# The per-query maxima of an fp32 attention block: from transposes on TensorE to 32x32 squares on VectorE, with one part of the conditioning moved inside the front

## The chip, the cores and the metric

The kernel runs on one core of one Trainium2 chip. The metric is the device time of one execution in microseconds (us), taken as the median of the runs. Everything is computed in fp32.

## The reference

One transformer block with adaptive layer norm, on x of shape (2, 2048, 576) with 16 heads of 36 channels and a hidden width of 2304:

```python
ada = silu(c) @ W_ada + b_ada                       # six parts of 576, one row per batch
shift_msa, scale_msa, gate_msa, shift_mlp, scale_mlp, gate_mlp = jnp.split(ada, 6, axis=-1)
h = modulate(layernorm(x), shift_msa, scale_msa)    # x * (1 + scale) + shift
qkv = h @ W_qkv + b_qkv
attn = softmax((q * 36**-0.5) @ k.T)                # per head, 2048 x 2048
x = x + gate_msa * ((attn @ v) @ W_proj + b_proj)
h = modulate(layernorm(x), shift_mlp, scale_mlp)
x = x + gate_mlp * (gelu(h @ W_fc1 + b_fc1) @ W_fc2 + b_fc2)
```

## The kernel before

**The front** (lines 174 to 592) computes queries, keys and values of batch 0 in four stages of 512 tokens (`queries_keys_values`). Each stage is a generator: its matmuls stand in half-steps between `yield`s (a query/key pair `pq` of two 128-column groups is two half-steps, a value tile `pv` is one). Between the half-steps one step of another generator, `later` (line 517), is taken. `later` works off what is not needed at once: parts 2, 5, 3 and 4 of the conditioning. Part 2 is `gate_msa`, the third of the six. For a part, `load_ada` brings 576 columns of `W_ada` to SBUF (tile `wa`, DMAs on SyncE's queue), `cleared` zeroes a PSUM tile `pa` with VectorE, `rows_of` (line 418) multiplies (line 425) and copies out, and `gates` spreads the row over 128 partitions by two more matmuls (line 475). After that `later` scales the projection and MLP weights by the gates (`gated`, DMAs on GpSimd's queue).

**The main part** is one loop over slots `G` (line 1332), in an order written out by hand: every instruction of compute is kept in program order on its engine. A round (class `Unit`, number u) is one head with 512 queries: 8 blocks of 512 queries x 16 heads = 128 rounds. A round has four groups of 512 keys (NG = 4), one group per slot, and g = G mod 4 is the slot's place in its round. A slot issues, in this order:

- `scores` of the round two rounds ahead (AHEAD = 8 slots): 8 matmuls into two PSUM tiles `s` (line 648; the pool `ps_s` has two), and `keep`, two ScalarE copies of them to SBUF tiles `e` (line 661).
- `fill`: other matmul work, one or two steps at a time, chosen by a running credit: projections of batch 1 (`pq_q`, `pv_q`), the output projection of a finished block (`po`), the MLP (`pf`, line 1172, and `py`, line 1220). Their last matmuls on 64 rows (line 104) are held back as `lasts`.
- `exps`: one ScalarE exponential over a group of the next slot (line 707).
- `weigh`: 8 matmuls of probabilities with values into the PSUM tile `av` (line 719). The pool `ps_v` holds one `av`, so the first `weigh` of a round (g = 0) waits until the previous round's `av` has been read.
- `maxima`: VectorE joins the group's scores into a running maximum `acc` (line 666), one or two `tensor_max` of 1,024 elements; in the last group a third of 512 elements (recorded under line 666 too) joins the two halves, and `acc[:, :512]` then holds, for each of 128 partitions, a maximum per query.
- `less`: VectorE subtracts the maximum `m` from a group (line 703, 2,048 elements), two slots ahead of its `weigh`; it is what `subtract(G + 2)` calls.
- `done`s: what takes the filled PSUM tiles out, on VectorE or ScalarE.
- at g = 3, `take` (lines 731 and 732): ScalarE copies the first half of `av` to `up`, VectorE adds the second half. This is what sets `av` free.

The 128 partition maxima of a query must still be joined. `turn` (line 678) does four TensorE transposes of 128x128 into a third `s` tile, called `mt`; `across` (line 691) reduces them with VectorE (`mx`, line 694), sends 2 KB to DRAM (`m_d`, line 695) and reads them back to all partitions (`m`, line 698), both on SyncE's queue. The two stand in the slot after the last group, g = 0, which the loop calls the chain slot: the order there is subtract, `turn`, `lasts`, `weigh`, `across`, maxima. At g = 2 the maxima stand ahead of the subtract, in the other slots after it.

Of the kernel before, what the change touches and what calls it, by code (L numbers as in the profile page):

```python
# [10 lines left out]
F32 = mybir.dt.float32  # L11
AF = mybir.ActivationFunctionType
ALU = mybir.AluOpType
AX = mybir.AxisListType
# [3 lines left out]
P = 128  # L18
# [4 lines left out]
def dit_block_kernel(  # L23
# [16 lines left out]
    nc = tc.nc  # L40
# [9 lines left out]
    QB = 512  # L50
    NQB = L // QB
    TB = QB // P
# [4 lines left out]
    NG = HALF // (2 * P)  # L57

    def seq(ins):

        return tc.keep_in_program_order(ins)
# [112 lines left out]
    with ExitStack() as front:  # L174
# [200 lines left out]
        def load_in(n):  # L375
# [141 lines left out]
        def later():  # L517

            was[2] = load_ada(2)
            was[5] = load_ada(5)  # L520
            lines = ap.tile([P, C], F32, name="lines")
            for b in range(B):
                for i, src in enumerate((b_fc2, b_proj)):
                    at = ds(64 * b + 32 * i, 1)
                    seq(nc.gpsimd.dma_start(out=lines[at, :], in_=src.unsqueeze(0)))
            yield
            yield
            yield
            pas[2] = cleared(2)
            yield  # L530
            g1 = []
            yield from gates(2, g1)
            was[3] = load_ada(3)
            pas[5] = cleared(5)
            yield
            g2 = []
            yield from gates(5, g2)
            was[4] = load_ada(4)
            half = [ap.tile([P, C], F32, name=f"half_{b}") for b in range(B)]
            for b in range(B):  # L540
# [26 lines left out]
            t = rows_of(4)  # L567
            yield
            modulation(4, t)()
# [27 lines left out]
    NU = NB * H  # L597

    with ExitStack() as main_part:
# [3 lines left out]
        ps_s = pool("ps_s", 2, space=PSUM)  # L603
# [3 lines left out]
        np_ = pool("n", 2)  # L607
# [4 lines left out]
        class Unit:  # L612
# [50 lines left out]
            def maxima(self, g):  # L663

                one, two = (self.es[g][:, j].rearrange("p i n -> p (i n)") for j in range(2))
                top = lambda out, x, y: seq(nc.vector.tensor_max(out, x, y))  # L666
                if g == 0:
                    self.acc = np_.tile([P, 2 * QB], F32, tag="acc", name=f"acc_{self.u}", bufs=1)
                    top(self.acc, one, two)
                    return  # L670
                a = self.acc
                top(a, a, one)
                top(a, a, two)
                if g == NG - 1:
                    self.am = a[:, :QB]
                    top(self.am, a[:, :QB], a[:, QB:])

            def turn(self):

                room = ps_s.tile([P, 2, 512], F32, tag="s", name=f"mt_{self.u}")  # L680
                self.pt = room[:, 0, :].rearrange("p (i n) -> p i n", i=TB)
                for i in range(TB):
                    seq(
                        nc.tensor.transpose(  # L684
                            self.pt[:, i, :],
                            self.am.rearrange("p (n i) -> p i n", i=TB)[:, i, :],
                            ident,
                        )
                    )

            def across(self):

                mx = np_.tile([P, TB], F32, tag="mx", name=f"mx_{self.u}")
                seq(nc.vector.tensor_reduce(out=mx, in_=self.pt, op=ALU.max, axis=AX.X))  # L694
                seq(nc.sync.dma_start(out=m_d[self.u], in_=mx))
                self.m = np_.tile([P, QB], F32, tag="m", name=f"m_{self.u}")
                flat = m_d[self.u].rearrange("p i -> (p i)")
                seq(nc.sync.dma_start(out=self.m, in_=flat.partition_broadcast(P)))

            def less(self, g):  # L700
# [590 lines left out]
        units = [Unit(u) for u in range(NU)]  # L1291
        AHEAD = 2 * NG
# [19 lines left out]
        def subtract(G):  # L1312
            if 0 <= G < NU * NG:
                units[G // NG].less(G % NG)
# [17 lines left out]
        for G in range(-AHEAD, NU * NG + 1):  # L1332
            u, g = divmod(G, NG)
            state["slot"] = G

            su, sg = divmod(G + AHEAD, NG)
            if sg == 0 and su + 1 < NU:
                units[su + 1].load_keys()
            if g == 1 and -1 <= u and u + 1 < NU:
                units[u + 1].load_values()  # L1340
            cu, cg = divmod(G - 1 + AHEAD, NG)
            chain = cg == NG - 1 and 0 <= cu < NU
            count(RATE)
            forced = g % 2 == 0 or G < 0 or credit > RATE
            tiles = units[su].scores(sg) if su < NU else None
# [8 lines left out]
            if 0 <= G + 1 < NU * NG:  # L1354
                lu, lg = divmod(G + 1, NG)
                units[lu].exps(lg)
            if chain:
                subtract(G + 2)
                units[cu].turn()
            for last in lasts:  # L1360
                last()
            lasts.clear()
            if 0 <= G < NU * NG:
                units[u].weigh(g)
            if chain:
                units[cu].across()
                if tiles:
                    units[su].maxima(sg)
            elif g == NG - 2:
                if tiles:  # L1370
                    units[su].maxima(sg)
                subtract(G + 2)
            else:
                subtract(G + 2)
                if tiles:
                    units[su].maxima(sg)
# [76 lines left out]
```

## Time and profile before

| | |
|---|---|
| median of 3 runs | 3703.63 us (3703.1 to 3707.89) |
| the profiled execution | 3707.24 us, span 3705.5 us |
| busy in the span | PE 3682.3, PEld 1722.0, DVE 2948.0, ACT 2327.3, POOL 706.2 us |
| granted TensorE clock | 0.999 of full speed |
| front, up to the first scores | 269.7 us |
| mean round, from one `mx` to the next | 24.73 us, of which VectorE is busy 21.49 us |
| tail after the last `mx` | 265 us |

PE is TensorE's matmuls, PEld its weight loads, DVE VectorE, ACT ScalarE, POOL GpSimd, SP SyncE. A row of a timeline is: start in us, length in us, engine, line, operation, written tile <- read tiles, shapes, and xN for N instructions merged into one row; in brackets the idle time of the engine ahead of it, and what ended it. An fp32 matmul appears as two instructions. The start of the next row tells what a row costs its engine, since rows overlap at their ends.

### The profile page before, as it was taken

To read this page: it belongs to the slowest core of one execution; us is meant where nothing else is said; L and a number is where in the kernel's file an instruction comes from. 1 tells how busy PE (TensorE), PEld (TensorE's weight loads), DVE (VectorE), ACT (ScalarE), POOL (GpSimd) and SP (SyncE) were. 2 spreads that over 40 slices of the span, in tenths; PEclk is the share of its full clock that TensorE was granted. 3 is DMA by queue.
4 is the path that set the end of the run, shared out by engine and by line. 5 is a ranking of instruction groups with operands and counts; after the bars stand their busy time and mean duration, and the time that the engine had idled before them with its cause. 6 is when DMAs were issued, how large, how long until landed. Compare 5 with 4: busy or idle time off the path is not lost.

```text
span 3705.5 us, 59239 instructions
## 1 busy us (share of the span) xinstructions
PE 3682.3 (99%) x23926; PEld 1722.0 (46%) x23926; DVE 2948.0 (80%) x3000; ACT 2327.3 (63%) x2166; POOL 706.2 (19%) x1044
## 2 busy tenths in 40 slices
PE   8999999999999999999999999999999999999999
PEld 4554344444444534454444444453444444444565
DVE  4627889889888888888889888988889888988422
ACT  0006767668776677667667777767667767676321
POOL 0101121222122111311131212211130213111411
PEclk9999999999999999999999999999999999999999
DMA  7733333544244343524353424424352435342522
GB/s 245 267 110 105 100 99 96 119 116 111 67 109 112 76 90 80 126 66 99 79 133 70 113 65 114 108 60 105 76 126 67 99 82 120 80 97 61 136 71 70
DMA packets 426946, 382.13 MB, mean 103 GB/s; under 512 B 315591, under 2 KB 316633, under 8 KB 426673
## 3 DMA queue, kind: packets, MB, share of 16 engines
q0 software_dynamic: 77248, 205.28, 20.5%
q1 hardware_dynamic: 82928, 129.54, 12.5%
q10 hardware_dynamic: 266496, 43.53, 7.2%
q8 instruction: 189, 3.10, 0.4%
q14 instruction: 85, 0.69, 0.1%
HBM read 306.98 MB, written 71.21 MB: 102 GB/s over the span
## 4 chain that ended last, share of the span: by engine, by line
PE 94%; DMA 3%; DVE 1%; ACT 1%; issue 1%; POOL 0%; SPq 0%; DVEq 0%; ACTq 0%; POOLq 0%
PE av L719 23%; PE s L648 22%; PE py L1220 15%; PE pf L1172 14%; PE po L799 4%; PE pq_q L975 3%; PE pq L278 3%; PE pf L104 2%; PE pv L328 2%; PE pv_q L799 2%; PE mt L684 2%; DMA x_b<-gp_d 1%; PE po L104 1%; DMA wa<-in_L_cond_W_ada_dram 1%; DVE acc L666 0%
## 5 line engine op out<-in xcount | busy, mean ns | idle before, releaser
L661 ACT COPY e<-s 128x1024 f32<-128x1024 f32 x1024 | 990.2, 1025 | 813.3 <-PE s L648 802.7
L703 DVE TENSOR_TENSOR e<-e,m 128x2048 f32<-128x2048 f32 x512 | 1162.8, 2276 | 9.8 <-DMA m<-m_d 9.8
L666 DVE TENSOR_TENSOR acc<-acc,e 128x1024 f32<-128x1024 f32 x768 | 939.5, 1223 | 171.9 <-ACT e L661 127.7
L707 ACT ACTIVATE e<-e 128x2048 f32<-128x2048 f32 x512 | 991.2, 1936 | 0.9 <-DVE e L703 0.8
L719 PE MATMUL av<-e,v 64*64 64x512 f32 x8192 | 981.3, 594 | 0.1
L648 PE MATMUL s<-qT,kT 36*64 36x512 f32 x8192 | 973.4, 589 | 2.1 <-DVE mx L694 1.1
L1220 PE MATMUL py<-w,gT 128*128 128x288 f32 x2304 | 580.2, 410 | 0.0
L648 PEld LDWEIGHTS s<-qT,kT 36*64 36x64 f32 x8192 | 313.1, 133 | 571.3 <-issue 522.8
L719 PEld LDWEIGHTS av<-e,v 64*64 64x64 f32 x8192 | 296.0, 133 | 510.0 <-issue 460.3
L1172 PE MATMUL pf<-h_b,w_b 128*128 128x512 f32 x1152 | 530.7, 605 | 0.0
L1220 PEld LDWEIGHTS py<-w,gT 128*128 128x128 f32 x2304 | 432.4, 190 | 175.4 <-issue 37.2
L740 POOL DMA_DIRECT2D o_d<-up x128 | 109.3, 854 | 1969.8 <-DMA o_d<-up 1439.2
L1172 PEld LDWEIGHTS pf<-h_b,w_b 128*128 128x128 f32 x1152 | 208.2, 190 | 318.0 <-issue 303.7
L694 DVE TENSOR_REDUCE mx<-mt 128x4 f32<-128x512 f32 x128 | 88.2, 689 | 169.9 <-PE mt L684 169.9
L1183 ACT ACTIVATE gT<-pf,bias 128x512 f32<-128x512 f32 x144 | 99.1, 688 | 193.0 <-PE pf L104 132.7
L1192 DVE SCALAR_TENSOR_TENSOR th<-th,gT 128x1024 f32<-128x1024 f32 x72 | 88.1, 1223 | 90.0 <-ACT th L1190 89.8
L666 DVE TENSOR_TENSOR acc<-e 128x1024 f32<-128x1024 f32 x128 | 155.6, 1216 | 4.4 <-ACT e L661 4.4
L1232 DVE TENSOR_TENSOR x_b<-py,x_b 128x288 f32<-128x288 f32 x192 | 81.5, 452 | 84.2 <-PE py L1220 84.2
L741 POOL DMA_DIRECT2D sum_d<-up x128 | 144.0, 1125 | 1.0 <-issue 1.0
L799 PE MATMUL po<-wpr_p,oT 128*128 128x288 f32 x512 | 132.6, 413 | 0.0
L278 PE MATMUL pq<-hT,w_in 128*128 128x512 f32 (+1 forms) x320 | 129.2, 555 | 0.0
L766 POOL DMA_DIRECT2D w_b<-in_L_cond_W_fc_dram x72 | 73.8, 1025 | 266.9 <-PE pf L1172 242.9
(156 smaller groups left out, 2453.2 us busy)
## 6 DMA issues: line engine op xcount, KB each, us to landing
w<-w_d POOLq DMA_DIRECT2D x72, 576.0 KB, 6.1
v<-v_d ACTq DMA_DIRECT2D x128, 296.0 KB
kT<-qk_d SPq DMA_DIRECT2D x256, 144.0 KB
w_b<-in_L_cond_W_fc_dram POOLq DMA_DIRECT2D x72, 512.0 KB, 4.6
m<-m_d SPq DMA_DIRECT2D x128, 256.0 KB
qT<-qk_d SPq DMA_DIRECT2D x256, 72.0 KB
w_d<-wg POOLq DMA_DIRECT2D x12, 864.0 KB, 8.4
qk_d<-ev SPq DMA_DIRECT2D x36, 256.0 KB
```

What stands on the lines that cost most here:

```text
L104: nc.tensor.matmul(outs[r][ts(c, 64), :], lhsT=lefts[r][:, ts(c, 64)], rhs=rights[r], start=starts[r], stop=not starts[r],)
L278: nc.tensor.matmul(pq[:, r, :n], lhsT=w_in[:, kc, cols], rhs=hT[:, kc, at], start=(kc == 0 and not (two and r)), stop=(kc == KC - 2 and tw ...
L648: nc.tensor.matmul(s[ts(c, 64), i, :], lhsT=self.kT[at, ds((2 * g + j) * P + 64 * c, 64)], rhs=self.qT[at, :], start=True, stop=True,)
L661: seq(nc.scalar.copy(self.es[g][:, j], s))
L666: top = lambda out, x, y: seq(nc.vector.tensor_max(out, x, y))
L703: seq(nc.vector.tensor_sub(e, e, m))
L707: seq(nc.scalar.activation(e, e, AF.Exp))
L719: nc.tensor.matmul(self.av[ts(i, 64), r, :], lhsT=self.v[ts(r, 64), ds((c + i * (HALF // P)) * HA, 64)], rhs=e[ts(r, 64), j, i, :], start= ...
L741: seq(nc.gpsimd.dma_start(out=sums, in_=hi[0:1, :], accum_op=ALU.add))
L799: nc.tensor.matmul(outs[n][:, :C2], lhsT=src[:, kc, ts(i, P)], rhs=w_[:, kc, ts(n, C2)], start=(kc == 0), stop=False,)
L1172: nc.tensor.matmul(pfs[j], lhsT=wc[:, kc, ts(j, P)], rhs=h2[:, kc, :], start=(kc == 0 and j == 0), stop=(kc == KC - 2 and j == 1),)
L1220: nc.tensor.matmul(py[n][:, :C2], lhsT=gTs[f - f % 2][:, f % 2, ts(i, P)], rhs=w2s[f - f % 2][:, f % 2, ts(n, C2)], start=(j == 0), stop=( ...
```

## The change

`turn` and the chain slot go. `maxima` calls `across` itself as soon as the last group is joined, at g = 3, ahead of `take`. `across` now does everything on VectorE, inside the tile `acc`:

```diff
                 if g == NG - 1:
-                    self.am = a[:, :QB]
-                    top(self.am, a[:, :QB], a[:, QB:])
+                    top(a[:, :QB], a[:, :QB], a[:, QB:])
+                    self.across(a)
...
-            def turn(self):
-                room = ps_s.tile([P, 2, 512], F32, tag="s", name=f"mt_{self.u}")
-                self.pt = room[:, 0, :].rearrange("p (i n) -> p i n", i=TB)
-                for i in range(TB):
-                    seq(nc.tensor.transpose(self.pt[:, i, :],
-                        self.am.rearrange("p (n i) -> p i n", i=TB)[:, i, :], ident))
-            def across(self):
-                mx = np_.tile([P, TB], F32, tag="mx", name=f"mx_{self.u}")
-                seq(nc.vector.tensor_reduce(out=mx, in_=self.pt, op=ALU.max, axis=AX.X))
-                seq(nc.sync.dma_start(out=m_d[self.u], in_=mx))
+            def across(self, a):
+                v = a[:, QB:].rearrange("p (i n) -> p i n", n=32)
+                seq(nc.vector.transpose(v, a[:, :QB].rearrange("p (n i) -> p i n", n=32)))
+                n16 = QB // 32
+                mq = a[:, :n16]
+                seq(nc.vector.tensor_reduce(out=mq, in_=v, op=ALU.max, axis=AX.X))
+                m4 = a[:32, n16 : 5 * n16].rearrange("p (r i) -> p r i", r=4)
+                for r in range(4):
+                    seq(nc.vector.tensor_copy(m4[:, r], mq[ts(r, 32), :]))
+                mx = np_.tile([32, n16], F32, tag="mx", name=f"mx_{self.u}")
+                by_query = m4.rearrange("p r i -> p i r")
+                seq(nc.vector.tensor_reduce(out=mx, in_=by_query, op=ALU.max, axis=AX.X))
+                flat = m_d[self.u].rearrange("p i -> (p i)")
+                seq(nc.sync.dma_start(out=flat.rearrange("(n i) -> n i", n=32), in_=mx))
                 self.m = np_.tile([P, QB], F32, tag="m", name=f"m_{self.u}")
-                flat = m_d[self.u].rearrange("p i -> (p i)")
                 seq(nc.sync.dma_start(out=self.m, in_=flat.partition_broadcast(P)))
```

The transpose turns each 32x32 square by itself, so that each quarter of 32 partitions comes to hold its own maximum of query 16p + i in partition p. Four copies bring the quarters side by side into the first 32 partitions, and a last reduction over four joins them. In the loop, `chain`, the early subtract of the chain slot and the two calls are taken out:

```diff
-            if chain:
-                subtract(G + 2)
-                units[cu].turn()
             for last in lasts:
                 last()
...
-            if chain:
-                units[cu].across()
-                if tiles:
-                    units[su].maxima(sg)
-            elif g == NG - 2:
+            if g == NG - 2:
```

In the front, `later` has two more `yield`s ahead of `pas[2] = cleared(2)`, so that part 2, and all that follows it in `later`, stands two half-steps later:

```diff
             yield
             yield
             yield
+            yield
+            yield
             pas[2] = cleared(2)
```

On the queues this moves, in each round, the store of the maxima and the read back: on SyncE they now stand ahead of the next `load_keys` (tiles `kT`, `qT`) instead of behind it. On VectorE, `take`'s add (line 732) now stands behind `across`. On TensorE only the transposes leave; in the front the ten matmuls of part 2 move behind two half-steps of `pq`, and those of parts 5, 3 and 4 move with them.

More of the change, by code (lines that the diff above doesn't have):

```diff
@@ L674, in maxima @@
                 if g == NG - 1:
-                    self.am = a[:, :QB]
-                    top(self.am, a[:, :QB], a[:, QB:])
-            def turn(self):
-                room = ps_s.tile([P, 2, 512], F32, tag="s", name=f"mt_{self.u}")
-                self.pt = room[:, 0, :].rearrange("p (i n) -> p i n", i=TB)
-                for i in range(TB):
[L683 to L689, printed above, removed]
-            def across(self):
-                mx = np_.tile([P, TB], F32, tag="mx", name=f"mx_{self.u}")
-                seq(nc.vector.tensor_reduce(out=mx, in_=self.pt, op=ALU.max, axis=AX.X))
-                seq(nc.sync.dma_start(out=m_d[self.u], in_=mx))
+                    top(a[:, :QB], a[:, :QB], a[:, QB:])
[14 more added lines that the diff above has]
+                seq(nc.sync.dma_start(out=flat.rearrange("(n i) -> n i", n=32), in_=mx))
                 self.m = np_.tile([P, QB], F32, tag="m", name=f"m_{self.u}")
-                flat = m_d[self.u].rearrange("p i -> (p i)")
                 seq(nc.sync.dma_start(out=self.m, in_=flat.partition_broadcast(P)))
@@ L1340, in dit_block_kernel @@
                 units[u + 1].load_values()
-            cu, cg = divmod(G - 1 + AHEAD, NG)
-            chain = cg == NG - 1 and 0 <= cu < NU
             count(RATE)
```

## The prediction

> **What bounds the kernel now.** I read the page's busy times and its chain of waits first, then the groups that the change touches, and then the timelines of TensorE and VectorE around the end of a round, since shares over the whole span cannot say what a stage is worth.
>
> ```profile
> PE 3682.3 (99%) x23926; PEld 1722.0 (46%) x23926; DVE 2948.0 (80%) x3000; ACT 2327.3 (63%) x2166; POOL 706.2 (19%) x1044
> PE av L719 23%; PE s L648 22%; PE py L1220 15%; PE pf L1172 14%; PE po L799 4%; PE pq_q L975 3%; PE pq L278 3%; PE pf L104 2%; PE pv L328 2%; PE pv_q L799 2%; PE mt L684 2%; DMA x_b<-gp_d 1%; PE po L104 1%; DMA wa<-in_L_cond_W_ada_dram 1%; DVE acc L666 0%
> L694 DVE TENSOR_REDUCE mx<-mt 128x4 f32<-128x512 f32 x128 | 88.2, 689 | 169.9 <-PE mt L684 169.9
> ```
>
> TensorE is the chain nearly everywhere, and the transposes `mt` are on it. VectorE's 80% looks like room, but between 300 and 3440 us it is busy 2728.7 of 3140 us, 87%, and the idle time in front of the removed reduction is no room that TensorE grants: it is VectorE waiting for the transposes.
>
> TensorE around the end of two rounds, first at 2004 to 2024 us, then at 1755 us:
>
> ```profile
> 2006.26 4.15 PE L799 MATMUL po<-wpr_p,oT 128*128 128x288 f32 x16
> 2010.25 0.63 PE L684 MATMUL mt<-ident,acc 128*128 128x128 f32 x4
> 2010.81 0.72 PE L104 MATMUL po<-wpr_p,oT 64*64 64x288 f32 x8
> 2011.34 1.90 PE L719 MATMUL av<-e,v 64*64 64x512 f32 x16
> ...
> 2018.33 4.15 PE L799 MATMUL po<-wpr_p,oT 128*128 128x288 f32 x16
> 2022.40 0.72 PE L104 MATMUL po<-wpr_p,oT 64*64 64x288 f32 x8
> ...
> 1759.09 0.63 PE L684 MATMUL mt<-ident,acc 128*128 128x128 f32 x4
> 1759.65 1.95 PE L719 MATMUL av<-e,v 64*64 64x512 f32 x16
> ```
>
> VectorE at the same two places:
>
> ```profile
> 2007.54 0.69 DVE L666 TENSOR_TENSOR acc<-acc 128x512 f32<-128x512 f32 x1
> 2008.15 0.68 DVE L732 TENSOR_TENSOR up<-up,av 128x512 f32<-128x512 f32 x1
> ...
> 1755.24 0.69 DVE L666 TENSOR_TENSOR acc<-acc 128x512 f32<-128x512 f32 x1
> 1755.85 0.68 DVE L732 TENSOR_TENSOR up<-up,av 128x512 f32<-128x512 f32 x1
> 1756.45 2.28 DVE L703 TENSOR_TENSOR e<-e,m 128x2048 f32<-128x2048 f32 x1
> 1759.76 0.69 DVE L694 TENSOR_REDUCE mx<-mt 128x4 f32<-128x512 f32 x1 [1.02 <-PE mt L684]
> ```
>
> The reader is to see two things. With transposes the way from `po` to its last matmuls takes 4.55 us (2006.26 to 2010.81), without them 4.07 us (2018.33 to 2022.40). And the add that sets `av` free, L732, ends at 2008.83, and TensorE needs `av` at 2011.34: 2.51 us of slack now. The change puts `across` into just this gap.
>
> **TensorE's transposes, removed.** 0.48 us per round (4.55 - 4.07) x 128 = 61.4 us; the chain's own share, 1.6% of 3705.5, says 59. With them go waits of TensorE at the third `s` tile: 3.0 us for `acc`, 1.9 us for ScalarE's copies, 1.1 us of `s` behind `mx`, together 6.0 us. Nothing takes their place on TensorE.
>
> **The front.** TensorE waits for part 2's weights:
>
> ```profile
> 34.00 3.70 PE L278 MATMUL pq<-hT,w_in 128*128 128x512 f32 x8
> 40.81 3.66 PE L425 MATMUL pa<-wa,cT 128*2 128x288 f32 x20 [3.11 <-DMA wa<-in_L_cond_W_ada_dram]
> ...
> 59.33 2.11 PE L425 MATMUL pa<-wa,cT 128*2 128x288 f32 x20
> ```
>
> 3.11 us ahead of them, and the matmuls stretch to 3.66 us where part 5's take 2.11: 4.7 us in all. In the new order two half-steps of `pq` come first, some 7 to 8 us of work (44.40 to 49.31, and a second half-step of 3.5), so from 37.7 TensorE reaches part 2 at about 45.5, when the weights, used up by 44.4 before, are there. Its cover is that `w_in`'s columns have landed: they were issued at 10 to 14 us, `wa`'s at 29. If not, the wait only moves, and the gain is nil. The later steps of `later` slide by two half-steps; what they prepare (scaled weights, the last two parts) is first read hundreds of us on, and the DMAs keep their order on each queue. I take 4.7 us, bounds 0 and 4.7.
>
> **VectorE's chain, added.** The links wait for each other, so their full lengths count. No row shows a transpose on VectorE. Of 512 elements, one source: the like-sized rows take 0.69 us (the half join, L694); two elements at a time, from the 128x128 copy of 222 ns, would make it 0.42; each element twice, 1.22 (the 1,024-element rows). I take 0.69, the row of the same size. The reduction of 512 to 16: 0.69, as L694. Four copies of 32x16: six small writes of `mod` (L458) stand in 0.79 us, 0.13 each, and a dependent small step in the `rstd` chain costs 0.20; so 0.5 to 1.0, taken 0.60. The last reduction: 0.16 for the smallest row (L397) and about 56 more elements, 0.22. Four hand-overs of 0.03, less the 0.08 by which a following independent row starts early: together 2.3 us from the end of the join to the start of the add, bounds 1.7 and 3.3.
>
> Against it stands the reduction removed, 0.60 us start to start, but that stood behind the add. So VectorE's work grows by 1.7 us a round: 21.5 + 1.7 = 23.2 in a round that would shrink to 24.25. On the mean it fits, at 96%.
>
> [...]
>
> **The new wait.** Behind `across` on VectorE are queued the add of `take`, the next subtract, the next maxima and the evictions; for the add waits TensorE's first `weigh` of the next round. I read the slack, from the end of L732 to the next `av`, for every round. It is 0.05 to 6.77 us, median 3.26; 40 of 127 rounds have less than 2.8. What happens in a round is: add's delay = 2.3 + 0.1 (it used to start 0.08 before the join's end) + carry, less what the add waited for ScalarE anyway (about 1.0 in some rounds); stall = delay + 0.48 (TensorE comes earlier) - slack, if positive. The carry into the next round is the delay + 0.48, less the stall, less 0.60, less VectorE's idle time up to the next join. In the block from 1690 to 2090 us, where `pf`, `py` and `po` follow each other, the slacks are 3.27, 3.11, 3.12, 3.25, 5.66, 4.17, 1.78, 1.77, 6.76, 5.66, 2.85, 3.11, 2.51, 3.35, 4.75, 5.50 and 1.16. The second has a carry of 1.12 (the round has 1 us of idle time): 2.41 + 1.12 + 0.48 - 3.11 = 0.9 of stall. The rounds stall 0.9, 1.3, 0.2, 1.3, 1.9, 1.4, 0.2 and 1.7 us, the others nothing: 8.9 in the block. `py` fills of 6 us hide the chain, a `pf` or `po` slot does not. The other blocks, done alike, give 5 to 8, the first 600 us 14: 56 us in all. The same sum gives 27 us for a chain of 1.7, 40 for 2.0, 77 for 2.6, 107 for 3.0 and 134 for 3.3.
>
> **The queues.** On SyncE the keys' load now waits for `across` and for the store of the maxima, which takes 1.4 to 7.1 us to be followed by its read back. The load then goes out some 8 to 15 us later, and the scores that need it come four slots, about 24 us, after the old issue: it stays hidden, priced at nothing; with no cover left each late load would stop TensorE by some 3 us (72 KB land in 2.7 us on GpSimd's queue, by the page's issues). `m` itself is ready earlier than before (VectorE waits 9.8 us for it today). GpSimd's queue is not touched in the main part.
>
> **Sum.** 3707.2 - 61.4 - 6.0 - 4.7 + 56 = 3691 for an execution like the profiled one, 16 us less; that one lies 3.6 us above the median of the runs, so from 3703.6 I come to 3688.
>
> **Rivals.** *Slower: the chain is long.* If the links cost 2.6 us and more, the add sets the pace in most `pf` and `po` slots, and stalls eat more than the 72 us gained; the point is a chain of 2.53 us. At 3.0 the result is 3703.6 - 72 + 107 = 3739. For it: seven dependent steps, one of a kind that the trace does not show, and 0.23 us is all that parts me from this point. Against it: rows of equal size.
> *Much faster: the add is not awaited.* With a chain of 1.7 us or less stalls are 27 or fewer: 3703.6 - 72 + 27 = 3659, and 3632 if none is left. For it: half of the rounds have over 3.2 us of slack, and 170 us of VectorE's waiting go. Against it: the dozen rounds with under 1.2 us of slack stall in any case.
> *No change.* Between 2.4 and 2.6 gain and stall cancel: 3704.
>
> **How the numbers follow.** A measurement tells some 0.2%, 7.4 us, from no change. The forecast, chains from 1.7 to 2.4, 0.45; much faster 0.12; no change 0.16; slower 0.27. Faster is then 0.57. The range runs from the chain of 1.7 with a few us less of stall to one of 2.8 (3703.6 - 72 + 91): 3655 to 3722; the faster cases' own range is 3632 to 3696.
>
> **What would show it.** Right: the chain from the join's end to the start of `take`'s add takes 2.0 to 2.5 us; TensorE gains a named wait of its first `av` of a round for `up`, absent behind `py`; no `mt`; the first `pa` wait of part 2 gone; VectorE at 90 to 96% in the middle. Wrong: a transpose far from 0.69 us, `s` waiting for keys, or TensorE waiting for `e` instead, which would mean that VectorE is late with its subtracts.

## The result and the profile after

The changed kernel takes 3758.29 us (median of 4 runs, 3755.58 to 3761.62) against 3704.76 us before (4 runs on the same chip): a ratio of 1.0141, 95% interval 1.0125 to 1.0157. It is slower by 53.5 us, where the forecast was 3688 us; sign and size were both missed. The profiled execution has a span of 3754.3 us.

The page of the kernel after, its engines, its chain by engine and by line, and the groups of the first `weigh` and of the new transpose:

```profile
PE 3646.8 (97%) x23414; PEld 1639.6 (44%) x23414; DVE 3203.7 (85%) x3768; ACT 2329.2 (62%) x2166; POOL 705.8 (19%) x1044
PE 58%; DVE 27%; issue 8%; DMA 4%; ACT 2%; POOL 1%; SPq 0%; DVEq 0%; POOLq 0%; ACTq 0%
PE av L719 13%; PE py L1220 13%; DVE acc L668 12%; PE s L650 12%; DVE e L703 7%; PE pf L1172 7%; PE pq L278 3%; DVE acc L685 2%; PE pq_q L975 2%; PE po L799 2%; PE pv L328 2%; PE pv_q L799 1%; DVE acc L688 1%; DVE acc L691 1%; DMA o_d<-up 1%
L719 PE MATMUL av<-e,v 64*64 64x512 f32 x8192 | 994.6, 601 | 89.4 <-DVE up L732 89.0
L685 DVE STREAM_TRANSPOSE acc<-acc 128x512 f32<-128x512 f32 x128 | 135.9, 1062 | 4.4
```

TensorE was the chain nearly everywhere; now 27% of the chain is VectorE's. 89.0 us of idle time stand in front of `av`, released by `take`'s add (L732). The transpose takes 1,062 ns.

VectorE in one round of the kernel after (start, duration, instruction):

```profile
2040.01 0.69 DVE L668 TENSOR_TENSOR acc<-acc 128x512 f32<-128x512 f32 x1
2040.73 1.05 DVE L685 STREAM_TRANSPOSE acc<-acc 128x512 f32<-128x512 f32 x1
2041.82 0.69 DVE L688 TENSOR_REDUCE acc<-acc 128x16 f32<-128x512 f32 x1
2042.54 0.69 DVE L691 COPY acc<-acc 32x16 f32<-32x16 f32 x4
2043.26 0.25 DVE L694 TENSOR_REDUCE mx<-acc 32x16 f32<-32x64 f32 x1
2043.47 0.69 DVE L732 TENSOR_TENSOR up<-up,av 128x512 f32<-128x512 f32 x1
```

From the join's end (2040.70) to the add's start it is 2.77 us; the forecast took 2.3. TensorE in the same round:

```profile
2041.46 0.72 PE L104 MATMUL po<-wpr_p,oT 64*64 64x288 f32 x8
2044.21 2.91 PE L719 MATMUL av<-e,v 64*64 64x512 f32 x16 [2.04 <-DVE up L732]
2046.88 2.69 PE L650 MATMUL s<-qT,kT 36*64 36x512 f32 x16
2049.39 1.90 PE L719 MATMUL av<-e,v 64*64 64x512 f32 x16
```

TensorE waits 2.04 us for the add. That was foreseen as a kind of wait. Two things behind it were not. The smaller one: `av` starts 2.75 us behind the last `po` (2041.46 to 2044.21), where in the kernel before it was 0.53 (2010.81 to 2011.34). The stall thus costs 2.22 us, 0.18 more than the idle time, since the `av` that has waited starts without its overlap with the one ahead (that row is 0.72 us long, and the next otherwise starts 0.53 us after it). I call this the restart. The larger one: the same sixteen matmuls that take 1.90 us last 2.91, and the next sixteen 2.69. The longest stall shows why. First TensorE, then the stretches of 4 us around it (each row: from and to; its length; busy us and instructions of PE, PEld, DVE, ACT, POOL; the granted clock; the DMA share; GB/s):

```profile
418.01 3.69 PE L719 MATMUL av<-e,v 64*64 64x512 f32 x16 [5.48 <-DVE up L732]
421.48 3.64 PE L650 MATMUL s<-qT,kT 36*64 36x512 f32 x16
```

```profile
416.00:420.00 4.00, 1.99 (x12) 0.78 (x16) 3.89 (x8) 1.79 (x4) 0.00 (x0) 0.61 0.31 106
420.00:424.00 4.00, 4.00 (x20) 1.00 (x19) 3.50 (x4) 0.47 (x1) 0.00 (x0) 0.50 0.63 186
424.00:428.00 4.00, 4.00 (x28) 1.28 (x24) 2.45 (x2) 3.36 (x3) 2.48 (x3) 0.61 0.21 20
```

After the stall the granted clock is half for some 10 us (0.39, 0.50 and 0.39 missing of three stretches of 4 us), and matmuls take about twice as long: 3.69 us for sixteen `av` and 3.64 for sixteen `s`, which take 1.90 at full clock. From the first scores to the last matmul, the kernel after has eight stretches at a clock of 0.50, 41.0 us together, so 20.5 us of clock are missing; 19.4 of them fall on time in which TensorE works. The kernel before has one such stretch, 1.7 us missing. In the kernel after, the slow stretches follow eight stalls of 1.93 to 5.48 us, and none of the shorter ones; eight other stalls of 2.0 to 2.4 us brought none.

What tells the two kinds apart is where a stall lies. The slow stretches are 3.41, 6.83 or 10.24 us long, and within each trace that has several they all begin on one grid of 3.413 us, to within 0.01 us. Here are two stalls of the kernel after of nearly the same length, 2042.17 to 2044.21 and 2143.67 to 2145.73; each row is a cell of this grid:

```profile
2041.65:2045.06 3.41, 1.37 (x16) 0.38 (x14) 3.27 (x9) 0.00 (x0) 0.00 (x0) 1.00 0.01 3
2045.06:2048.47 3.41, 3.41 (x20) 1.05 (x16) 3.41 (x5) 0.00 (x0) 0.00 (x0) 0.50 0.66 171
2144.05:2147.46 3.41, 1.73 (x16) 0.67 (x20) 3.33 (x7) 0.34 (x1) 0.00 (x0) 1.00 0.60 97
2147.46:2150.87 3.41, 3.41 (x36) 1.23 (x32) 3.41 (x4) 2.21 (x3) 0.00 (x0) 1.00 0.49 141
```

The first stall lies within one cell, which is idle for 2.04 us, and the next cell runs at half clock. The second is cut by the end of a cell into 0.38 and 1.68 us, and the clock stays full. Of the eight stalls with slow clock behind them seven put 2.04 us or more into one cell and the eighth 1.29; those without put in 1.80 at most. Over the 17 traces, in the cells at full clock behind the first scores: all 129 with 2.0 us or more of idle time are followed by half clock, 11 of the 17 with 1.9 to 2.0, 42 of the 311 with 1.0 to 1.9, and none of the 16,557 with less. What decides between 1.0 and 2.0 us stays open. The grid stands differently against the program in each execution (its first line lies 0.47 us behind the span's start in this trace, 0.57 in the one before, 2.19 in that of x2_place), so whether a stall of some 2 us brings half clock is luck.

**The bill.** From the profiled executions (span 3705.5 before, 3754.3 after: +48.8 us). The first scores start at 264.89 instead of 269.65 us: -4.8. From there to the end it is +53.6. TensorE's idle time between matmuls (gaps over 0.2 us) goes from 7.0 to 93.7 us: +86.7. The clock, where TensorE works: 19.4 - 1.7 = +17.7. The restarts, by which a matmul starts later than its idle time accounts for, against the same sequence of eight matmuls without a stall: +7.0. What is left, 53.6 - 86.7 - 17.7 - 7.0 = -57.8, is what the absent transposes are worth. The kernel before says the same by itself: in 122 of its rounds the way over the transposes can be set against the same way without them, and the difference is 0.47 us in each, 59.9 us in 128 rounds.

### The profile page after: what moved, and what is told of

It is laid out like the page before. It is cut to its first block, busy times and chain, and to the rows that moved or that the text cites. A ratio compares the mean times of both kernels' runs of the same rounds, so it can differ in the third digit from the quotient of the medians.

```text
span 3754.3 us, 58832 instructions
## 1 busy us (share of the span) xinstructions
PE 3646.8 (97%) x23414; PEld 1639.6 (44%) x23414; DVE 3203.7 (85%) x3768; ACT 2329.2 (62%) x2166; POOL 705.8 (19%) x1044
## 4 chain that ended last, share of the span: by engine, by line
PE 58%; DVE 27%; issue 8%; DMA 4%; ACT 2%; POOL 1%; SPq 0%; DVEq 0%; POOLq 0%; ACTq 0%
PE av L719 13%; PE py L1220 13%; DVE acc L668 12%; PE s L650 12%; DVE e L703 7%; PE pf L1172 7%; PE pq L278 3%; DVE acc L685 2%; PE pq_q L975 2%; PE po L799 2%; PE pv L328 2%; PE pv_q L799 1%; DVE acc L688 1%; DVE acc L691 1%; DMA o_d<-up 1%
## 5 line engine op out<-in xcount | busy, mean ns | idle before, releaser
L719 PE MATMUL av<-e,v 64*64 64x512 f32 x8192 | 994.6, 601 | 89.4 <-DVE up L732 89.0
L685 DVE STREAM_TRANSPOSE acc<-acc 128x512 f32<-128x512 f32 x128 | 135.9, 1062 | 4.4
```

Source lines behind the costliest of these rows:

```text
L685: seq(nc.vector.transpose(v, a[:, :QB].rearrange("p (n i) -> p i n", n=32)))
L719: nc.tensor.matmul(self.av[ts(i, 64), r, :], lhsT=self.v[ts(r, 64), ds((c + i * (HALF // P)) * HA, 64)], rhs=e[ts(r, 64), j, i, :], start= ...
```

## Experiments

All ratios are to the kernel before, on the same chip, with 95% intervals.

**x1_front.** The kernel before, with the front's edit alone:

```diff
+            yield
+            yield
             pas[2] = cleared(2)
```

> The kernel before with the two more yields in the front alone. The first scores started at 269.65 us before and at 264.89 us after; if the front's gain stands by itself, this kernel is 4.8 us faster than before (some 3700 us), with 264.9 us at its first scores. If the gain only moves the wait, nothing changes.

Measured: 3703.81 us, 0.9991 [0.9981, 1.0], 10 runs. The gain of 4.8 us seen in the trace's front lies within the interval (0 to 7 us). The traces measure it more finely: from the first `pq` to the first scores it is 248.4 us in the kernel before and 243.7 in each of the 16 kernels with this edit, 4.7 us less. What hides this in the run times is the start ahead of that `pq`, which takes 20.6 to 26.3 us in the traces. This part is not what made the kernel slower.

**x2_place.** The chain stands in the slot after the last group, behind the add and a subtract:

```diff
                     top(a[:, :QB], a[:, :QB], a[:, QB:])
-                    self.across(a)
...
-            if g == NG - 2:
+            cu, cg = divmod(G - 1 + AHEAD, NG)
+            if cg == NG - 1 and 0 <= cu < NU:
+                subtract(G + 2)
+                units[cu].across(units[cu].acc)
+                if tiles:
+                    units[su].maxima(sg)
+            elif g == NG - 2:
```

> The changed kernel with the same VectorE work, but the chain put where the old reduction stood: in the slot after the last group, behind take's add and behind the subtract. Theory A (the chain stands between the join and the add that sets av free): the waits of av for up fall from 89 us to the carry alone, 29 us by the same round-by-round bookkeeping with a chain of 2.77 us; with the transposes, their waits and the front gone (72 us) that is 3705 - 72 + 29 = 3662 us, a few us more if some restarts are slow. Rival B (VectorE's total work, 93% busy in the middle, is the bound wherever it stands): about 3750 us, with waits of TensorE elsewhere.

Measured: 3708.06 us, 1.0006 [0.9996, 1.0015], between the two expectations. The place accounts for some 51 of the 53.5 us (2.4 are left on this chip), but does not bring the gain that was forecast. TensorE's waits in this kernel (what waits, for whom; us in all, times, longest):

```profile
PE av L718 <- DVE up L731: 39.2, 32, 2.8
PE po L798 <- DVE x_b L1108: 5.2, 3, 2.6
PE py L1219 <- DVE x_b L1108: 2.9, 1, 2.9
```

The add still comes late in 32 rounds, though it is ahead of its own round's chain: the chain's time is carried over to the next join. Between the end of the chain and such a late add lie 16 to 23 us, and VectorE is idle for 0.6 of them in the median. Evictions of `po` and `py` are late more often now. The clock's loss is 12.0 us.

**x3_noturn.** The changed kernel without the transpose; the order of its instructions is otherwise the same:

```diff
-                seq(nc.vector.transpose(v, a[:, :QB].rearrange("p (n i) -> p i n", n=32)))
```

> The changed kernel without the 32x32 transposes; the reduction reads the other half of acc instead, so the maxima are not those of the queries. The chain is then 2.77 - 1.09 = 1.68 us. If the bookkeeping of slack and carry was right and only the transpose was mis-sized, the waits are 26 us and the time 3705 - 72 + 26 = 3659 us, the figure that the prediction gives for a chain of 1.7. If something else stops TensorE, such as the m or key loads standing in another order, it stays above 3690 us.

Measured: 3674.49 us, 0.9914 [0.9899, 0.9929]. With a chain shorter by 1.1 us `av` waits 29.3 us; the bookkeeping of the prediction, run with the shorter chain, says 26. And the clock's loss is 1.7 us only. So the transpose alone costs the change 84 us, of which 60 are waits for `up` and 18 the clock.

**x4_short, x8_halves, x7_flat: why the transpose takes 1.06 us.** Bfloat16 squares; two transposes of 256 elements; squares of neighbouring columns. The edits in that order:

```diff
+                    top(self.m.bitcast(mybir.dt.bfloat16)[:, :QB], a[:, :QB], a[:, QB:])
...
+                seq(nc.vector.transpose(v, b[:, :QB].rearrange("p (n i) -> p i n", n=32)))
```

```diff
+                squares = a[:, :QB].rearrange("p (n i) -> p i n", n=32)
+                for r in range(2):
+                    seq(nc.vector.transpose(v[:, ts(r, 8), :], squares[:, ts(r, 8), :]))
```

```diff
-                seq(nc.vector.transpose(v, a[:, :QB].rearrange("p (n i) -> p i n", n=32)))
+                seq(nc.vector.transpose(v, a[:, :QB].rearrange("p (i n) -> p i n", n=32)))
```

> The changed kernel with the joined maxima written in bf16 and the 32x32 squares turned in bf16, so the maxima are rounded; everything else as in the changed kernel. If the 1.06 us of the transpose come from the four bytes of an element (two cycles each), it takes 0.55 us here, the chain 2.25 us, the waits 53 us, and the time is 3705 - 72 + 53 = 3686 us and some us of slow restarts. If the time of a transpose goes by elements alone, nothing changes and it is 3758 us.

> The changed kernel with the transpose cut in two of 256 elements each, which gives the fixed and the running part of its price. Two cycles an element and next to no fixed part: 0.53 to 0.6 us each, the pair about as long as the one, 3758 us and a little more. One cycle an element and a fixed half microsecond: 0.8 us each, the chain 0.55 us longer, 114 us of waits by the bookkeeping instead of 89 and some 3790 us.

> The changed kernel with the squares read as runs of 32 neighbouring elements instead of elements 16 apart, so the maxima go to other queries than their own. If the stride of the read is what makes the transpose 1.06 us, it falls to 0.6 us or so, the chain to 2.3 us and the time to about 3695 us. If a transpose costs two cycles an element anyway, nothing changes: 1.06 us and 3758 us.

Measured: 3767.28 us (1.0166 [1.0151, 1.0181]), 3766.23 us (1.0161 [1.0141, 1.0182]) and 3728.53 us (1.006 [1.0039, 1.008]). The group of the transpose in each, in the same order:

```profile
L687 DVE STREAM_TRANSPOSE m<-m 128x512 bf16<-128x512 bf16 x128 | 142.1, 1110 | 4.4
```

```profile
L687 DVE STREAM_TRANSPOSE acc<-acc 128x256 f32<-128x256 f32 x256 | 143.4, 599 | 4.4
```

```profile
L685 DVE STREAM_TRANSPOSE acc<-acc 128x512 f32<-128x512 f32 x128 | 91.1, 711 | 4.4
```

Half the width does not shorten it (1,110 ns); half the length nearly halves it (599 ns), and the two halves together take 0.14 us more than the whole. So neither the four bytes nor a fixed part explains the 1.06 us; the order of reading does. Columns 16 apart cost 1,062 ns, neighbouring ones 711, close to the 0.69 us of the prediction. Yet x7_flat is still 24 us slower than before (its two runs 20 and 28; of the 28, 5 lie in the start ahead of the first `pq`): the duration taken for the transpose, had it been right, would not have saved the forecast.

**x6_twice.** The transpose done twice:

```diff
                 seq(nc.vector.transpose(v, a[:, :QB].rearrange("p (n i) -> p i n", n=32)))
+                seq(nc.vector.transpose(v, a[:, :QB].rearrange("p (n i) -> p i n", n=32)))
```

> The changed kernel with each transpose done twice, which is one more 1.06 us link in the chain: 3.86 us. The bookkeeping of slack and carry gives 186 us of waits for it, 3705 - 72 + 186 = 3819 us. If TensorE's slow restarts after stalls of about 2 us and more are a cost of their own (some 20 us in the changed kernel), most of the stalls now are that long, and the time lies well above that, at 3860 us or more, with a mean granted clock under 0.99. If they are not, it is 3819 us within 10.

Measured: 3904.43 us, 1.0534 [1.0513, 1.0555]; mean clock 0.980.

```profile
PE av L720 <- DVE up L733: 172.4, 83, 6.6
```

The waits double, from 89 to 172 us, but the clock's loss goes from 20.5 to 78.5: a cost of its own, as expected of the second theory.

**x9_free.** x2_place, with ScalarE emptying both halves of `av`:

```diff
-                seq(nc.vector.tensor_add(self.up, self.up, self.av[:, 1, :]))
+                seq(nc.scalar.copy(self.m, self.av[:, 1, :]))
+                seq(nc.vector.tensor_add(self.up, self.up, self.m))
```

> As x2_place, and av is set free by ScalarE alone: it copies both halves to SBUF, the second one into the round's m tile, which is dead by then, and VectorE adds them from there. VectorE's work is that of x2_place. If the waits left in x2_place (39 us of av for up) come from the add's place in VectorE's queue, they are gone, and the time is some 3655 to 3670 us, faster than both kernels. If VectorE's total work is what is left as the bound, the wait turns up elsewhere (e not subtracted in time, the evictions of py and po late) and the time stays above 3690 us.

Measured: 3704.31 us, 1.0 [0.999, 1.001]. The wait for `up` is gone (2.8 us, for ScalarE's copy), but `po` and `py` wait 34.0 us for VectorE's evictions, and the clock loses 22.2 us. What VectorE has too much of seems to have come back at another tile; but VectorE itself waits 17.7 us, in 26 rounds, for ScalarE's second copy in front of the add (8.3 us for the first copy in x2_place), so part of the late evictions may be due to that, and no run here separates the two.

**x10_turned, x11_scatter, x12_free_flat.** x2_place with neighbouring columns; a second, small transpose or the store's order puts the queries right. x12_free_flat is x9_free with the edit of x11_scatter:

```diff
+                top_q = a[:32, 128 : 128 + 32]
+                seq(nc.vector.tensor_reduce(out=top_q[:, :n16], in_=by_query, op=ALU.max, axis=AX.X))
+                mx = self.m[:32, :32]
+                seq(nc.vector.transpose(mx, top_q))
+                seq(nc.sync.dma_start(out=flat.rearrange("(i n) -> i n", n=32), in_=mx[:n16, :]))
```

```diff
-                seq(nc.sync.dma_start(out=flat.rearrange("(n i) -> n i", n=32), in_=mx))
+                seq(nc.sync.dma_start(out=flat.rearrange("(i n) -> n i", n=32), in_=mx))
```

> As x2_place (the chain stands in the slot after the last group, 3708 us), but the squares are read from 32 neighbouring columns (711 ns in x7_flat, 1,050 ns strided); the maxima then lie with the query's low bits on the partition, and one more turn of a single 32x32 square puts them back, so the output is the reference's. A (VectorE's length is the price, by waits and by the slow clock that long waits bring): 0.34 us less and about 0.15 us more (the smallest rows) a round; from the change to x7_flat 0.35 us brought 30 us, so 0.19 us should bring 10 to 16: 3692 to 3698 us, av's waits for up near 30 us instead of 39. B (in this placement VectorE's load no longer matters and only the place did): 3705 to 3711 us. The turn of the small square is not in any row yet: if it takes 0.3 us or more, nothing is left of the gain.

> As x10_turned, without the second turn: the store of the maxima puts them in order instead, 512 pieces of 4 bytes where 32 of 64 bytes were. A: 0.34 us less on VectorE, some 25 to 30 us less than x2_place: 3678 to 3685 us, av's waits near 25 us. B (the store with its 512 small pieces takes so long that m comes late): VectorE's subtracts wait for m, the scores' slots follow, and the time is above 3700 us; the row to read is the idle time of the subtract line in front of m, 10 us or less in the runs so far.

> As x9_free (ScalarE copies both halves of av out, 3704 us), with the neighbouring columns and the store of 4-byte pieces as in x11_scatter. A: VectorE was the bound there through the evictions (po and py waited 34 us for x_b), 0.34 us of 23 a round is 43 us of VectorE's time; if half of it reaches TensorE, 3675 to 3685 us. B (the evictions wait for ScalarE's copies in front of the add and not for VectorE's total): 3698 to 3706 us.

Measured: 3699.58 us (0.9986 [0.9976, 0.9996]), 3830.04 us (1.0345 [1.033, 1.0361]) and 3824.02 us (1.0328 [1.0313, 1.0344]). x10_turned falls a little short of its first expectation: the small transpose takes 199 ns, and 31.9 us of waits and 20.5 us of lost clock are left. The other two went to theory B of x11_scatter, as the subtract's group in x11_scatter shows:

```profile
L702 DVE TENSOR_TENSOR e<-e,m 128x2048 f32<-128x2048 f32 x512 | 1163.3, 2277 | 114.1 <-DMA m<-m_d 113.9
```

The subtracts wait 113.9 us for `m`: a store in pieces of 4 bytes is late. x12_free_flat has the same wait (120.2 us), so it says nothing on its own question.

**x13_shared.** VectorE turns and reduces the squares behind the add; TensorE turns the 128x16 rest:

```diff
+            def squares(self):
+                a = self.acc
+                v = a[:, QB:].rearrange("p (i n) -> p i n", n=32)
+                seq(nc.vector.transpose(v, a[:, :QB].rearrange("p (i n) -> p i n", n=32)))
+                self.mq = a[:, : QB // 32]
+                seq(nc.vector.tensor_reduce(out=self.mq, in_=v, op=ALU.max, axis=AX.X))
             def turn(self):
...
+                self.pt = room[: QB // 32, 0, :P]
+                seq(nc.tensor.transpose(self.pt, self.mq, ident))
...
                 units[u].take()
+            if tiles and sg == NG - 1:
+                units[su].squares()
```

> The work shared: VectorE turns the 32x32 squares (read from 32 neighbouring columns, 0.70 us) and reduces them (0.69), right behind take's add, so that the add is not behind it; then TensorE turns the 128x16 rest with one transpose where it had four, behind the first weigh of the round, and VectorE's last reduction of 128 elements (0.25) puts the maxima straight into the query's order. The four copies across the quarters and the second turn are gone. The front's later part is in. A (what cost the change its gain is the add of av behind a chain, the load of VectorE and the slow clock after single long stalls): TensorE saves 0.36 of its 0.48 us a round, 46 us, and 4 of the front; VectorE has 1.0 us more a round instead of 2.0; no av waits for up, at most 15 us of waits elsewhere, and the clock's loss stays below 8 us: 3660 to 3680 us. B (any lengthening of VectorE's round, wherever it stands, comes back as evictions and scores that wait): like x10_turned, 3695 to 3710 us, with waits over 40 us.

Measured: 3699.35 us, 0.9985 [0.9975, 0.9995], the time that B gave. Yet A's conditions on the waits nearly hold: `av` waits for `up` 6.3 us where none was expected, idle time is 14.3 us in all, and no clock is lost behind the first scores. What does not hold is TensorE's saving: the bill leaves only -10.5 us for three transposes in four. The rows say why. From sixteen `av` to the `s` behind them TensorE takes 2.08 us with this transpose and 1.72 without, so the one of 128x16 between these two costs 0.37 us a round, where the four cost 0.47. To get all of the gain (53 to 61 us in the table below, with no transpose on TensorE), TensorE has to do none.

**x16_vector, x14_pool, x15_scalar.** No transpose on TensorE, neighbouring columns, the chain up to the copies right behind the add and ahead of the subtract; the last reduction and the small transpose stand behind the subtract. The four copies run on VectorE, GpSimd (there the rest stands behind the next maxima) and ScalarE. The edit against x13_shared, and the line that differs in x14_pool (in x15_scalar it is `nc.scalar.copy`):

```diff
+                for r in range(4):
+                    seq(nc.vector.tensor_copy(self.m4[:, r], mq[ts(r, 32), :]))
...
+                seq(nc.vector.tensor_reduce(out=top_q[:, :n16], in_=by_query, op=ALU.max, axis=AX.X))
+                mx = self.m[:32, 192 : 192 + 32]
+                seq(nc.vector.transpose(mx, top_q))
...
-                units[cu].turn()
                 subtract(G + 2)
                 units[cu].across()
```

```diff
-                    seq(nc.vector.tensor_copy(self.m4[:, r], mq[ts(r, 32), :]))
+                    seq(nc.gpsimd.tensor_copy(self.m4[:, r], mq[ts(r, 32), :]))
```

> As x10_turned with all of the maxima on VectorE and no transpose on TensorE, but the order on VectorE is that of x13_shared: join, take's add, the turn of the squares, the reduction and the four copies, and only then the subtract; the last reduction and the small turn come behind it. VectorE's work a round is that of x10_turned (2.0 us more than in the kernel before), only its place differs. A (load: what VectorE has too much of comes back in TensorE's waits wherever it stands): 40 to 50 us of waits, 15 to 20 us of slow clock, 3695 to 3705 us. B (place: the waits of x10_turned come from a chain that stands behind a subtract, late in the slot): waits under 25 us, clock loss under 8, 3660 to 3680 us.

> As x16_vector, with the four copies across the quarters on GpSimd, so that VectorE has 1.2 us a round more than in the kernel before instead of 2.0; the last reduction and the small turn stand behind the maxima of the next unit, as GpSimd's queue is slower. A (load decides): waits like x13_shared's 14 us and clock loss below 5, and TensorE's 53 us are kept: 3655 to 3670 us. B (GpSimd's queue is behind with its DMA issues of 0.9 and 1.1 us, so VectorE waits for the copies, or m comes late): VectorE's reduction shows idle time for GpSimd or the subtracts for m, above 60 us in all, and the time is 3690 us or more.

> As x16_vector, with the four copies on ScalarE (busy 63% of the span before). A (load of VectorE decides): as x14_pool, 3655 to 3675 us. B (ScalarE's copies of the scores are what TensorE's s tiles wait for, and four small operations of some 0.2 us in front of them push these): s waits for e by 30 us or more, 3690 us or more.

Measured: 3687.43 us (0.9945 [0.9927, 0.9962]), 3692.91 us (0.9976 [0.9965, 0.9988]) and 3764.2 us (1.0157 [1.0142, 1.0172]). x16_vector is the fastest full kernel here, 17.7 us below the one before (3705.14 on that chip). TensorE's first waits of its main part in x10_turned and x16_vector, two kernels with the same work on VectorE:

```profile
PE av L720 <- DVE up L733: 31.9, 30, 2.9
```

```profile
PE av L723 <- DVE up L736: 23.6, 24, 2.4
```

Place and load both count: moving the chain ahead of the subtract saves 11 us (17.7 less 6.6, each against the kernel before on its chip), by the waits (idle time 47 to 39 us) and by the clock (20.5 to 12.0); these two are from the profiled executions, which lie 15.9 us apart. The time, the idle time and the clock's loss all fall between A's expectation and B's. Taking 0.7 us of copies off VectorE did not help, since both engines gave it back, by their rows in x14_pool and x15_scalar:

```profile
DVE m L697 <- POOL m L690: 82.3, 127, 5.7
```

```profile
PE s L650 <- ACT e L663: 41.5, 54, 3.5
PE av L723 <- ACT e L711: 33.9, 42, 0.8
```

VectorE waits for GpSimd's copies in 127 rounds; and with the copies on ScalarE, the scores' tiles and the exponentials are late. What a VectorE with less to do would give is thus not shown. x14_pool shows the clock by itself: its ten runs are one program, and go from 3690.8 us at a mean clock of 0.997 to 3706.4 us at 0.993. Four thousandths of 3,700 us are 14.8 us; the runs differ by 15.6.

**The bill over the runs.** Each row against the profiled execution of before, in us, from the first scores to the end: change of the time, of TensorE's idle time, of the clock lost while it works, of the restarts, and what is left for the transposes.

| kernel | first scores to end | idle | clock | restarts | left |
|---|---|---|---|---|---|
| after | +53.6 | +86.7 | +17.7 | +7.0 | -57.8 |
| x1_front | -3.5 | -1.4 | -1.7 | +0.0 | -0.4 |
| x2_place | +2.9 | +47.7 | +10.0 | +4.7 | -59.4 |
| x3_noturn | -29.0 | +24.9 | +0.0 | +5.5 | -59.3 |
| x4_short | +63.1 | +88.6 | +25.4 | +6.9 | -57.8 |
| x6_twice | +201.8 | +174.9 | +73.8 | +10.1 | -57.0 |
| x7_flat | +25.1 | +66.7 | +11.3 | +6.6 | -59.5 |
| x8_halves | +62.5 | +91.9 | +21.2 | +7.1 | -57.6 |
| x9_free | +2.4 | +40.7 | +18.5 | +2.1 | -58.8 |
| x10_turned | +2.1 | +39.9 | +17.9 | +3.9 | -59.6 |
| x11_scatter | +126.2 | +118.9 | +62.1 | +6.1 | -61.0 |
| x12_free_flat | +123.9 | +121.5 | +50.6 | +5.7 | -54.0 |
| x13_shared | -3.5 | +7.3 | -1.7 | +1.3 | -10.5 |
| x14_pool | +0.6 | +39.8 | +19.0 | +2.2 | -60.4 |
| x15_scalar | +60.1 | +75.7 | +18.2 | +18.7 | -52.5 |
| x16_vector | -14.0 | +31.6 | +10.1 | +3.2 | -58.8 |

The times differ by 231 us, and what is left is 57 to 61 us in twelve of the fourteen kernels without transposes on TensorE, against the 59.9 read from the kernel before; in x12_free_flat it is 54 and in x15_scalar 53, so 6 to 7 us there are not accounted for. x1_front, which keeps the four transposes, has 0.4 left.

## Why the prediction was wrong

**The bound and the mechanism** were right. TensorE is no longer the chain everywhere; it waits for `up` with its first `av` of a round, in 59 places of 5.5 us at most; `mt` is gone. VectorE is busy 2934.2 of 3140 us in the middle, 93.4%, within the 90 to 96 said.

**The transposes, -61.4 us.** This term was right. The reading of one pair of rounds (4.55 against 4.07 us) holds in 122 rounds, 59.9 us in all, and the bill leaves 57.8. The waits at the third `s` tile, -6.0, did go: they are in the idle time before, 7.0 us.

**The front, -4.7 us.** Right as well: 4.7 us between the first `pq` and the first scores. Part 2 has no wait in front of it (its one row at 45.64 us takes 2.11):

```profile
45.64 2.11 PE L425 MATMUL pa<-wa,cT 128*2 128x288 f32 x20
```

**VectorE's chain, 2.3 us.** This is the first step that failed, and in it the transpose: 0.69 said, 1.06 measured, within the bounds (0.42 to 1.22) but far from the value taken; the prediction's own list of what would show it wrong has this first. Its links as said add up to 2.24 us rather than 2.3, which hardly matters. Reduction 0.69 as said; the four copies 0.72 from start to start, said 0.60; last reduction 0.25, said 0.22. The row of equal size misled, since its elements lie next to each other and the transpose's do not: x7_flat, which reads neighbours, takes 0.71.

**The stalls, +56 us.** The bookkeeping was sound: for the chain measured, 2.74 to 2.77 us, it gives 87 to 89 us, and the trace has 89.0. Without the transpose it says 26 against 29.3. The waits for `up` were mis-sized by their input alone, 33 us. The break-even point of 2.53 us, though, is refuted by x7_flat: its chain is 2.43 us (2028.69, the join's end, to 2031.12), and it is slower by 24 us. In its profiled execution the clock and the restarts cost 18 us beyond the idle time.

**What the sum lacked: the clock and the restarts.** This is the second step that failed: the sum priced a stall by its idle time alone, and put what a stall does to TensorE afterwards at nothing. That is 17.7 us of clock here, 73.8 in x6_twice, and 7.0 us of restarts. The rows of the kernel before had it. The prediction read that part 2's matmuls, behind a wait of 3.11 us, "stretch to 3.66 us where part 5's take 2.11", and counted this for the front without asking why. They stand in a stretch of half clock, 0.50 from 41.54 to 44.95 us, and the sixteen `av` behind the longest wait for `acc` take 3.45 us where they otherwise take 1.90, most of that time at a clock of 0.50 (2738.07 to 2741.48):

```profile
41.54:44.95 3.41, 3.41 (x13) 1.05 (x14) 0.44 (x1) 0.00 (x0) 0.00 (x0) 0.50 1.04 359
2737.12 0.72 PE L684 MATMUL mt<-ident,acc 128*128 128x128 f32 x4 [1.93 <-DVE acc L666]
2737.77 3.45 PE L719 MATMUL av<-e,v 64*64 64x512 f32 x16
```

In the kernel after, the clock behind the eight stalls is 0.50 too, and the slow stretches last one, two or three times 3.41 us. Five of these stalls were only 1.93 to 2.27 us long, and 2.0 us or more of idle time in one cell of 3.41 were followed by half clock in all 129 cases of the 17 traces. The grid stands differently in each execution, and with it what a stall of some 2 us brings: the one from 2042.17 us, within one cell, brought slow clock, the one from 2143.67, cut into 0.38 and 1.68 us, did not.

**The sum again.** With each term as measured: 3707.2 - 59.9 - 4.7 + 86.7 + 17.7 + 7.0 = 3754.0 us, where the profiled execution took 3756.1. Against the prediction's 3691 that is 1.5 from the transposes, 36.7 from the stalls (net of the 6.0 that sat at the `s` tile), 17.7 from the clock and 7.0 from the restarts; 2.1 us stay open.

**The rivals.** *Slower: the chain is long* came true in mechanism and place. Its price at 2.77 us would have been 3703.6 - 72 + 89 = 3721; the rest up to 3758 is mostly the clock and the restarts, which that price lacked too. *Much faster* had its case in x3_noturn: a chain of 1.7 us, 3674 where 3659 was said. The add is awaited by then in 38 rounds.

**The queues**, priced at nothing: no wait of `s` for keys shows in the trace, and the subtracts wait for `m` 1.0 us where they waited 9.8. As said.

## What to carry to other kernels

What the 57.8 us of work taken from TensorE were worth here went by the place and the length of the new work on VectorE: 53.5 us slower with the add behind the new chain, a ratio of 1.0006 with the add ahead of it (x2_place), and 17.7 us faster with neighbouring columns and the chain ahead of the subtract (x16_vector). So put the instruction that the bounding engine waits for ahead of the new chain, and count the chain's full length, carried over into the next round (39.2 us of waits are left in x2_place). Price a stall of TensorE above its own length: up to 0.18 us for the restart here, and, once it nears 2 us (1.93 was the shortest with half clock behind it in the kernel after), the chance of half clock behind it, read from the granted clock in the stretches behind the stalls that the kernel already has. Read the cost of a data movement from a row with the same order of access, not only the same size (1,062 against 711 ns here); where there is none, test at the far bound whether the sign holds.

## What was not expected of the hardware

- The transpose on VectorE takes 1,062 ns for 128x512 with columns 16 apart and 711 ns with neighbouring ones; in bf16 with columns 16 apart 1,110.
- Half clock comes in stretches of 3.41, 6.83 or 10.24 us on a grid of 3.413 us, and 2.0 us or more of idle time within one cell of the grid was followed by it in 129 of 129 cases (17 traces). The grid differs from execution to execution (its first line lies 0.57 us behind the span's start in the kernel before, 0.47 in the one after); between runs of one program (x14_pool) the cost varies by 15 us.
- A stalled `av` costs up to 0.18 us more than its idle time, 7.0 us over the kernel after.
- One transpose of 128x16 between `av` and `s` costs TensorE 0.37 us, four of 128x128 behind other work 0.47 us (x13_shared and the kernel before).
- A store of the same 2 KB in 4-byte pieces made VectorE wait 114 us for `m`, where 64-byte pieces made it wait 2.9 (x11_scatter and x2_place).
